# Seven-product attention on one core: the order of maxima, shifts, denominators and the first unit

## The chip, the core and the metric

The kernel runs on one core of a Trainium2 chip. The metric is the device time of one execution in microseconds (us); a comparison takes the median of several executions. Five engines work side by side, each through its own instructions in their written order: TensorE (PE in the profile, with weight loads as PEld), VectorE (DVE), ScalarE (ACT), GpSimd (POOL) and SyncE (SP), which issues most DMAs.

## The reference, cut to what matters

Input x has 4 batches of 256 channels on 64 x 64 points (N = 4096), in float32. A layer of self-attention is followed by a block of clustering, MLP and pointwise convolution:

```python
xf = x.reshape(B, C, N)                              # 4, 256, 4096
q = einsum("oc,bcn->bno", wq, xf) + bq               # 32 wide
k = einsum("oc,bcn->bon", wk, xf) + bk[None, :, None]
attn = softmax(einsum("bnd,bdm->bnm", q, k), axis=-1)
v = einsum("oc,bcn->bon", wv, xf) + bv[None, :, None]
x = gamma[0] * einsum("bcn,bmn->bcm", v, attn).reshape(B, C, H, W) + x
...
y = x + ls1 * cluster(group_norm(x))                 # 4 heads, 2 x 2 folds, 4 centres
y = y + ls2 * conv1x1(gelu(conv1x1(group_norm(y), w1, b1)), w2, b2)   # 256 -> 1024 -> 256
z = relu(batch_norm(y * dw_w))
out = relu(batch_norm(conv1x1(z, pw_w)))
```

The change touches the attention and the seam to what follows it.

## The kernel before

For each batch the 4096 queries are cut into 8 blocks `nb` of 512, and for each block the 4096 keys into 8 groups `g` of 512. A pair is a *unit* `u = 8 * nb + g`, so a batch has 64 units. A unit's scores, exponentials and products are kept in a tile `s` of four quarters (`B21, B11, B12, B22`). The product of exponentials and values is made by a scheme of Strassen's kind: seven products of quarter matrices instead of eight. `factors(u)` forms the sums of quarters that it needs (`t31` on VectorE, `s[:, B12]` and `t4s` on GpSimd), and with them the sums of the softmax's denominators (`acc`: `one` and `both`). `weigh(u, av, part)` (lines 646 to 670) issues the seven products in four parts, in the order that the tables `ORDER` and `LAST` (lines 44 and 45) give; `LAST` holds for a batch's last unit. Product 1 needs `s[:, B11]`, 2 and 3 `s[:, B21]` and `s[:, B22]`, 5 and 7 need `t31`, 6 `s[:, B12]`, and 4 `t4s`. Banks `av` 0 and 1 lie in `ps_a`, 2 and 3 in `ps_m`.

Everything is written by hand in one order per engine (`manual_schedule`); no scheduler moves anything. While unit `u` is weighed, `exps(u + 1)` subtracts the block's maximum (line 589, VectorE) and takes exponentials (lines 593 to 595, ScalarE), `factors(u + 1)` follows, and up to three half units of *scores* of about eleven units ahead are made (`half`, lines 458 to 475): two matmuls into a PSUM tile `sc`, a copy of it into `s` by ScalarE (`kept`, line 439), and a running maximum over keys by VectorE (`highest_of`, line 450). The scores' pool `ps_s` has two buffers, and one of them is `hold`, which keeps the maximum row and the exponentials of B12.

A block's maximum is finished in steps. `fold` (line 507) takes the maximum of the two halves of `top`; it was called by `due` (line 868), right after the last half unit of a block. `highest` (line 557, called at `g == 5`) transposes and reduces on VectorE, copies four small pieces on ScalarE (line 544), reduces and transposes once more, and sends the row through DRAM by two DMAs on SP's queue (`everywhere`); `known` (line 572) copies it into `hold` at `g == 6`. In `weighting` (line 878) the second and third steps of `highest` stood ahead of the maximum of the half unit that was made in the same part:

```python
if ripe:
    next(peak)
    mb = next(peak)
for f in maxima:
    f()
```

At the end of a block `evict` copies the four banks out on ScalarE and scales them with gamma; `combined` adds the quarters on GpSimd during the next block. The first product of the next block writes bank 0, which `evict` must have read. `total` and `leave` divide by the denominators. For the last block of a batch (`more` is false) this was different: `gather` (line 672) ran on GpSimd after three additions of `factors`, VectorE combined the evicted banks 0 and 1 and took banks 2 and 3 straight from PSUM (`complete`), and the denominators were summed over the partitions by four matmuls `den` (line 1005). Then follow a reciprocal, `seen` and `pooled` (statistics and cell sums of x), the division, `add_one`, and a group norm.

In the last ten units of a batch x is loaded again (`load`), v's bias is added on ScalarE (`shift`, line 760, two operations of 128 x 1024 each), and the attention's output is added to it by accumulating DMAs on GpSimd's queue (`back`, `back_one`), from `tail`. `shift` stood ahead of the first products of its unit.

Batch 0 has no predecessor to hide its start in: `alone` (line 803) makes projections and the first block's scores; `derived` makes twelve tiny VectorE operations for later stages, all in unit 0; `wf` turns a small weight.

Of the kernel before, what the change touches and what calls it, by code (L numbers as in the profile page):

```python
# [11 lines left out]
ALU = mybir.AluOpType  # L12
# [7 lines left out]
NBLK = N // NB  # L20
# [22 lines left out]

ORDER = (1, 5), (2, 3), (7, 6), (4,)
# [15 lines left out]
def attention_then_cluster_block(  # L60
# [179 lines left out]
    def derived():  # L240

        for s, e, g, m, b_ in (
            (dw_d, dw_e, "dw_g", "dw_m", "dw_b"),
            (pw_s, pw_e, "pw_g", "pw_m", "pw_b"),
        ):
            nc.vector.tensor_tensor(s, s, par(g), ALU.mult)
            nc.vector.tensor_tensor(e, s, par(m), ALU.mult)
            nc.vector.tensor_tensor(e, par(b_), e, ALU.subtract)
        nc.vector.tensor_tensor(dw_d, dw_d, par("dw_w"), ALU.mult)
        nc.vector.tensor_tensor(lsb1, par("ls2"), par("mlp_b2"), ALU.mult)  # L250
        nc.vector.tensor_tensor(lsb1, lsb1, dw_d, ALU.mult)
        nc.vector.tensor_tensor(dw_e, dw_e, lsb1, ALU.add)

        nc.vector.tensor_scalar(gbv, gbv, pvc("gamma"), None, ALU.mult)
        nc.vector.tensor_scalar(ab, pv_s[:, PV["alpha"] : PV["alpha"] + 2], 0.5, None, ALU.mult)

# [54 lines left out]
    def attention(b, xs, ys):  # L311
# [245 lines left out]
        def highest(nb):  # L557

            top = tops.pop(nb)
# [40 lines left out]
        def factors(u):  # L600
# [15 lines left out]
            plus(t4s[u], s[:, B12], s[:, B21])  # L616
            if g == 0:
# [28 lines left out]
        def weigh(u, av, part):  # L646
# [14 lines left out]
            for i in (ORDER if u < units - 1 else LAST)[part]:  # L661
# [10 lines left out]
        def gather(nb):  # L672

            acc = accs.pop(nb)
            rdens[nb] = work.tile([P, NB], F32, tag="rden", bufs=1, name=f"rden_{b}_{nb}")
            for h in range(2):
                plus(rdens[nb][:, h * QW : (h + 1) * QW], acc[:, 1 - h, 0], acc[:, 1 - h, 1])
# [18 lines left out]
        def combine(nb, eng):  # L696

            t = ts[nb]
            yield eng.tensor_tensor(t[:, 1], t[:, 1], t[:, 0], ALU.subtract)
# [3 lines left out]

        def combined(nb):

            t = ts[nb]
            yield from combine(nb, nc.gpsimd)
            yield nc.gpsimd.tensor_tensor(t[:, ::3], t[:, ::3], ts.pop((nb, 2)), ALU.add)
            yield nc.gpsimd.tensor_tensor(t[:, 1], ts.pop((nb, 3))[:, 0], t[:, 1], ALU.subtract)

        def complete(nb, av, c):

            t = ts[nb]
            dst, src, op = (
# [1328 lines left out]
```

## Time and profile before

| | us |
|---|---|
| median of 3 runs | 3188.45 (3188.23 to 3193.07) |
| time of the profiled execution | 3184.64 |
| its span, first to last instruction | 3182.5 |
| mean granted TensorE clock | 0.992 |
| span of one block of 8 units (187.58 to 245.02) | 57.44 |

| engine, line | what | count | mean ns |
|---|---|---|---|
| PE L664 | products of the weighing, 128x256 | 7168 | 380 |
| PE L426 | scores, 128x512 | 1024 | 467 |
| DVE L589 | subtraction of the maximum, 128x1024 | 512 | 1209 |
| DVE L450 | running maximum, 128x1024 from PSUM | 350 | 1219 |
| DVE L612 | t31, 128x1024 | 256 | 1218 |
| ACT L439 | copy of scores, 128x1024 | 512 | 1010 |
| ACT L760 | shift of x, 128x1024 | 32 | 1137 |
| POOL L598 | additions of 128x512 | 960 (the three largest groups and acc<-t,t) | 1296 to 1402 |

Busy times overlap, since the engines run side by side, and matmuls overlap each other (a mean of 380 ns stands for a new one each 216 ns). What counts is where the engine that is never done waits, and for whom; the views below show that.

### The profile page before, as it was taken

To read this page: it belongs to the slowest core of one execution; us is meant where nothing else is said; L and a number is where in the kernel's file an instruction comes from. 1 tells how busy PE (TensorE), PEld (TensorE's weight loads), DVE (VectorE), ACT (ScalarE), POOL (GpSimd) and SP (SyncE) were. 2 spreads that over 40 slices of the span, in tenths; PEclk is the share of its full clock that TensorE was granted. 3 is DMA by queue.
4 is the path that set the end of the run, shared out by engine and by line. 5 is a ranking of instruction groups with operands and counts; after the bars stand their busy time and mean duration, and the time that the engine had idled before them with its cause. 6 is when DMAs were issued, how large, how long until landed. Compare 5 with 4: busy or idle time off the path is not lost.

```text
span 3182.5 us, 41287 instructions
## 1 busy us (share of the span) xinstructions
PE 3049.3 (96%) x14210; PEld 2501.5 (79%) x14210; DVE 2489.0 (78%) x3569; ACT 1770.9 (56%) x2807; POOL 2315.4 (73%) x2223
## 2 busy tenths in 40 slices
PE   7999999999999999999999999999999999999999
PEld 5788887788678888878867888886877788875786
DVE  4888887777788887777778888777768888877675
ACT  4566664545556666354455666635555666644444
POOL 3888887377578888647758888855866888894663
PEclk9999999999999999999999999999999999999999
DMA  5122226200112113510011212441011112150000
GB/s 165 40 63 64 60 59 185 70 17 27 47 48 66 54 60 98 152 57 17 27 57 44 64 60 59 114 128 57 27 40 44 54 60 63 57 145 6 14 21 27
DMA packets 105873, 200.39 MB, mean 63 GB/s; under 512 B 14416, under 2 KB 30400, under 8 KB 104128
## 3 DMA queue, kind: packets, MB, share of 16 engines
q1 hardware_dynamic: 101856, 181.94, 18.1%
q0 software_dynamic: 2976, 14.70, 2.5%
q8 instruction: 113, 1.85, 0.3%
q10 hardware_dynamic: 832, 1.11, 0.1%
q14 instruction: 96, 0.79, 0.1%
HBM read 149.37 MB, written 48.34 MB: 62 GB/s over the span
## 4 chain that ended last, share of the span: by engine, by line
PE 63%; DVE 14%; POOL 12%; ACT 6%; issue 4%; DMA 1%; SPq 0%; ACTq 0%; POOLq 0%; DVEq 0%
PE av L664 25%; PE mo L1655 9%; PE sc L426 5%; POOL acc L598 5%; PE hq L1738 5%; DVE top L450 3%; DVE s L589 3%; PE hp L1738 3%; PE hr L1738 3%; PE fv L1227 3%; POOL t L598 3%; PE vp L381 2%; ACT s L439 2%; DVE t L612 2%; POOL s L598 1%
## 5 line engine op out<-in xcount | busy, mean ns | idle before, releaser
L439 ACT COPY s<-sc 128x1024 f32<-128x1024 f32 x512 | 514.3, 1010 | 458.1 <-PE sc L426 406.7
L589 DVE TENSOR_TENSOR s<-s,hold 128x1024 f32<-128x1024 f32 x512 | 598.9, 1209 | 8.4 <-ACT hold L572 5.1
L598 POOL TENSOR_TENSOR acc<-acc,t 128x512 f32<-128x512 f32 x416 | 543.7, 1328 | 0.0
L598 POOL TENSOR_TENSOR s<-t,s 128x512 f32<-128x512 f32 x256 | 344.7, 1347 | 268.2 <-DVE t L612 201.1
L664 PE MATMUL av<-s,v 128*128 128x256 f32 x2048 | 529.0, 381 | 10.9 <-ACT t L689 10.9
L664 PE MATMUL av<-t,v 128*128 128x256 f32 x2048 | 529.5, 381 | 4.7 <-DVE t L612 3.8
L664 PE MATMUL av<-s,sum 128*128 128x256 f32 x2048 | 527.3, 380 | 2.6 <-POOL s L598 2.4
L612 DVE TENSOR_TENSOR t<-s,hold 128x1024 f32<-128x1024 f32 x256 | 311.7, 1218 | 217.9 <-POOL acc L598 83.2
L426 PE MATMUL sc<-q,k 128*128 128x512 f32 x1024 | 392.3, 467 | 59.7 <-DVE top L450 38.8
L450 DVE TENSOR_TENSOR top<-sc,top 128x1024 f32<-128x1024 f32 x350 | 426.6, 1219 | 27.0 <-ACT s L439 22.5
L664 PEld LDWEIGHTS av<-s,v 128*128 128x128 f32 x2048 | 389.2, 190 | 73.6 <-ACT t L689 12.5
L664 PEld LDWEIGHTS av<-t,v 128*128 128x128 f32 x2048 | 390.4, 191 | 63.8 <-DVE t L612 5.4
L664 PEld LDWEIGHTS av<-s,sum 128*128 128x128 f32 x2048 | 389.2, 190 | 58.6 <-POOL s L598 5.8
L1693 ACT ACTIVATE hs<-hs,pv_s 128x256 f32<-128x256 f32 x496 | 232.6, 503 | 352.4 <-DVE hs L1729 352.4
L1655 PE MATMUL mo<-hs,w 128*128 128x256 f32 x1512 | 384.8, 381 | 0.0
L598 POOL TENSOR_TENSOR t<-s 128x512 f32<-128x512 f32 x256 | 331.8, 1296 | 58.2 <-PE av L664 46.6
L1655 PEld LDWEIGHTS mo<-hs,w 128*128 128x128 f32 x1512 | 283.8, 190 | 46.8 <-ACT hs L1693 6.1
L593 ACT ACTIVATE hold<-s 128x512 f32<-128x512 f32 x256 | 154.2, 602 | 255.8 <-DVE s L589 255.3
L426 PEld LDWEIGHTS sc<-q,k 128*128 128x128 f32 x1024 | 173.8, 189 | 144.2 <-DVE top L450 84.0
L595 ACT ACTIVATE s<-s 128x1024 f32<-128x1024 f32 x256 | 266.8, 1042 | 0.0
L1729 DVE TENSOR_TENSOR hs<-hq,hs 128x256 f32<-128x256 f32 x496 | 198.2, 420 | 86.3 <-PE hq L1738 76.3
L664 PE MATMUL av<-t,sum 128*128 128x256 f32 x1024 | 262.4, 378 | 0.0
(292 smaller groups left out, 4813.1 us busy)
## 6 DMA issues: line engine op xcount, KB each, us to landing
k<-k SPq DMA_DIRECT2D x256, 256.0 KB, 2.7
x<-in_x SPq DMA_DIRECT2D x62, 512.0 KB, 6.8
out<-xn SPq DMA_DIRECT2D x62, 256.0 KB, 2.1
att<-t SPq DMA_DIRECT2D x56, 256.0 KB, 3.8
x<-att POOLq DMA_DIRECT2D x12, 1024.0 KB, 9.7
q<-q SPq DMA_DIRECT2D x32, 256.0 KB, 4.0
w<-in_w SPq DMA_DIRECT2D x8, 1024.0 KB, 11.1
k<-hl_k SPq DMA_DIRECT2D x28, 256.0 KB, 2.6
```

Source lines behind the costliest of these rows:

```text
L426: nc.tensor.matmul(sc[:, r, :], k_s[:, (2 * h + r) * P : (2 * h + r + 1) * P], qs[u // GRP], start=True, stop=True,)
L439: nc.scalar.copy(slots[u][:, PAIR[h]].rearrange("p h r n -> p r h n"), tiles(sc))
L450: nc.vector.tensor_tensor(top, src, top if saved[nb] is None else saved[nb], ALU.max)
L589: nc.vector.tensor_tensor(sh, sh, mb.to_broadcast([P, 2, 2, QW]), ALU.subtract)
L595: nc.scalar.activation(s[:, PAIR[1]], s[:, PAIR[1]], AF.Exp)
L598: nc.gpsimd.tensor_tensor(out, x, y, op)
L612: nc.vector.tensor_tensor(t31[u], s[:, B11 : B22 + 1 : 2], b12.to_broadcast([P, 2, 2, QW]), ALU.add)
L664: nc.tensor.matmul(av[bank][:, half_ * QW : (half_ + 1) * QW], a[:, r], t[:, r], start=(g == 0 and r == 0 and i in (1, 7, 2, 4)), stop=(g ...
L1655: return nc.tensor.matmul(bank[:, half * HB : (half + 1) * HB], a[:, j], t, start=start, stop=stop)
L1693: nc.scalar.activation(src, src, AF.Gelu_apprx_tanh, bias=pvc("b1", P, j + 4 * (i > 1)))
L1729: nc.vector.tensor_tensor(dst, ps, term, ALU.add)
L1738: nc.tensor.matmul(out, w, x, start=True, stop=True)
```

## The change

Seven edits, all of order or of the engine that does a thing:

- The maximum of the half unit stands ahead of the second and third steps of `highest`.
- From block 2 on, `fold` is called by `highest`, so that it follows the next unit's subtractions.
- `shift` moves to the end of its unit, ahead of `tail`.
- In the last block of a batch VectorE sums the denominators: `factors` of the last unit adds `t31` and takes the difference on VectorE, `gather` adds `t4s` and the halves there too. Banks 2 and 3 are evicted by ScalarE; GpSimd makes the four combining additions and VectorE the last two.
- A table `FIRST` orders unit 0 of each batch: products 1 and 2, then 3 and 5.
- The twelve operations of `derived` are done one a unit from unit 16 on.
- In `alone`, `wf` and two pairs of v stand earlier, and the last maximum precedes its copy.

```diff
--- before.py
+++ after.py
@@ -41,6 +41,7 @@
 
 
 
+FIRST = (1, 2), (3, 5), (7, 6), (4,)
 ORDER = (1, 5), (2, 3), (7, 6), (4,)
 LAST = (1, 5), (7, 6), (2, 3), (4,)
 
@@ -239,21 +240,27 @@
 
     def derived():
 
+        def op(*a):
+            return lambda: nc.vector.tensor_tensor(*a)
+
+        def scale(*a):
+            return lambda: nc.vector.tensor_scalar(*a)
+
+        todo = []
         for s, e, g, m, b_ in (
             (dw_d, dw_e, "dw_g", "dw_m", "dw_b"),
             (pw_s, pw_e, "pw_g", "pw_m", "pw_b"),
         ):
-            nc.vector.tensor_tensor(s, s, par(g), ALU.mult)
-            nc.vector.tensor_tensor(e, s, par(m), ALU.mult)
-            nc.vector.tensor_tensor(e, par(b_), e, ALU.subtract)
-        nc.vector.tensor_tensor(dw_d, dw_d, par("dw_w"), ALU.mult)
-        nc.vector.tensor_tensor(lsb1, par("ls2"), par("mlp_b2"), ALU.mult)
-        nc.vector.tensor_tensor(lsb1, lsb1, dw_d, ALU.mult)
-        nc.vector.tensor_tensor(dw_e, dw_e, lsb1, ALU.add)
-
-        nc.vector.tensor_scalar(gbv, gbv, pvc("gamma"), None, ALU.mult)
-        nc.vector.tensor_scalar(ab, pv_s[:, PV["alpha"] : PV["alpha"] + 2], 0.5, None, ALU.mult)
-
+            todo.append(op(s, s, par(g), ALU.mult))
+            todo.append(op(e, s, par(m), ALU.mult))
+            todo.append(op(e, par(b_), e, ALU.subtract))
+        todo.append(op(dw_d, dw_d, par("dw_w"), ALU.mult))
+        todo.append(op(lsb1, par("ls2"), par("mlp_b2"), ALU.mult))
+        todo.append(op(lsb1, lsb1, dw_d, ALU.mult))
+        todo.append(op(dw_e, dw_e, lsb1, ALU.add))
+        todo.append(scale(gbv, gbv, pvc("gamma"), None, ALU.mult))
+        todo.append(scale(ab, pv_s[:, PV["alpha"] : PV["alpha"] + 2], 0.5, None, ALU.mult))
+        return todo
 
     def wf():
 
@@ -556,6 +563,7 @@
 
         def highest(nb):
 
+            fold(nb)
             top = tops.pop(nb)
             low = spare()[:, nb % 2]
             steps = reduced(top[:, 0], top[:, 1], low, ALU.max, nc.scalar.copy)
@@ -614,6 +622,10 @@
             )
             plus(s[:, B12], t31[u][:, 1], s[:, B11])
             plus(t4s[u], s[:, B12], s[:, B21])
+            if u == units - 1:
+                nc.vector.tensor_tensor(one, one, t31[u][:, 1], ALU.add)
+                nc.vector.tensor_tensor(both, both, one, ALU.subtract)
+                return
             if g == 0:
                 plus(both, s[:, B12], s[:, B21])
             else:
@@ -658,7 +670,7 @@
                 3: (2, 1, s4, s[:, B22]),
             }
 
-            for i in (ORDER if u < units - 1 else LAST)[part]:
+            for i in {0: FIRST, units - 1: LAST}.get(u, ORDER)[part]:
                 bank, half_, a, t = terms[i]
                 for r in range(2):
                     nc.tensor.matmul(
@@ -673,8 +685,13 @@
 
             acc = accs.pop(nb)
             rdens[nb] = work.tile([P, NB], F32, tag="rden", bufs=1, name=f"rden_{b}_{nb}")
+            eng = nc.vector if nb == NBLK - 1 else nc.gpsimd
+            if nb == NBLK - 1:
+                eng.tensor_tensor(acc[:, 1], acc[:, 1], t4s[units - 1], ALU.add)
             for h in range(2):
-                plus(rdens[nb][:, h * QW : (h + 1) * QW], acc[:, 1 - h, 0], acc[:, 1 - h, 1])
+                eng.tensor_tensor(
+                    rdens[nb][:, h * QW : (h + 1) * QW], acc[:, 1 - h, 0], acc[:, 1 - h, 1], ALU.add
+                )
 
         def evict(nb, av, i):
 
@@ -693,29 +710,16 @@
                 scale=pvc("gamma"),
             )
 
-        def combine(nb, eng):
+        def combined(nb, last=nc.gpsimd):
 
             t = ts[nb]
+            eng = nc.gpsimd
             yield eng.tensor_tensor(t[:, 1], t[:, 1], t[:, 0], ALU.subtract)
             yield eng.tensor_tensor(t[:, 3], t[:, 1], t[:, 3], ALU.subtract)
             yield eng.tensor_tensor(t[:, 1], t[:, 1], t[:, 2], ALU.add)
             yield eng.tensor_tensor(t[:, 2], t[:, 2], t[:, 3], ALU.add)
-
-        def combined(nb):
-
-            t = ts[nb]
-            yield from combine(nb, nc.gpsimd)
-            yield nc.gpsimd.tensor_tensor(t[:, ::3], t[:, ::3], ts.pop((nb, 2)), ALU.add)
-            yield nc.gpsimd.tensor_tensor(t[:, 1], ts.pop((nb, 3))[:, 0], t[:, 1], ALU.subtract)
-
-        def complete(nb, av, c):
-
-            t = ts[nb]
-            dst, src, op = (
-                (t[:, ::3], av[2].rearrange("p (h n) -> p h n", h=2), ALU.add),
-                (t[:, 1], av[3][:, :QW], ALU.subtract),
-            )[c]
-            nc.vector.scalar_tensor_tensor(dst, src, pvc("gamma"), dst, ALU.mult, op)
+            yield last.tensor_tensor(t[:, ::3], t[:, ::3], ts.pop((nb, 2)), ALU.add)
+            yield last.tensor_tensor(t[:, 1], ts.pop((nb, 3))[:, 0], t[:, 1], ALU.subtract)
 
         def total(nb):
 
@@ -820,10 +824,19 @@
                     halved("k", 1)
                     halved("q", 1)
                     rest = load_rest()
-                for h in range(2):
-                    half(u, h)()
+                half(u, 0)()
+                if u < GRP - 1:
+                    half(u, 1)()
+                else:
+
+                    sc = products(u, 1)
+                    highest_of(0, tiles(sc))
+                    kept(u, 1, sc)
+                    v_pair(14)
                 if u < 6:
                     v_pair(u + GRP)
+                elif u == 6:
+                    wf()
                 if u > 1:
                     next(rest, None)
             fold(0)
@@ -832,15 +845,12 @@
                     f()
             tp = turned_over(0, ps_m.tile([P, 4, P], F32, tag="m", name=f"tt_{b}_0"))
             half(GRP, 0)
-            v_half(28)
             dgs["dg"] = across(0, "w2", tp)
             spread(0, dgs["dg"])
+            v_pair(15)
             exps(0)
             factors(0)
-            v_half(29)
-            v_pair(15)
             half(GRP, 1, True)
-            wf()
             for f in sums(GRP - 1):
                 f()
 
@@ -871,8 +881,8 @@
                 return []
             p, h, kept_only = at[u, part]
             fs = [half(p, h, kept_only)]
-            if h and p % GRP == GRP - 1:
-                fs.append(lambda: fold(p // GRP))
+            if p == 2 * GRP - 1 and h:
+                fs.append(lambda: fold(1))
             return fs
 
         def weighting(next_x, fill, early, begin):
@@ -932,13 +942,11 @@
                 elif ripe:
                     peak = highest(nb + 1)
                     next(peak)
-                if u == 0:
-                    early()
+                if early and nb > 1:
+                    early.pop(0)()
                 if u in views:
                     pooled(views[u])
                     seen(views[u], (0,))
-                if u in shifts:
-                    shift(shifts[u])
                 weigh(u, av, 0)
                 if short:
                     two = ps_s.tile([P, 2, NB], F32, tag="s", name=f"tt_{b}_{nb + 1}")
@@ -954,28 +962,22 @@
                 if g == GRP - 1:
                     evict(nb, av, 0)
                     evict(nb, av, 2 if more else 1)
-                    if not more:
-                        for _ in combine(nb, nc.vector):
-                            pass
                 if g + 1 < GRP or more:
                     factors(u + 1)
                 if more and nb and g == GRP - 2:
                     known(mb)
+                for f in maxima:
+                    f()
                 if ripe:
                     next(peak)
                     mb = next(peak)
-                for f in maxima:
-                    f()
                 if (u, 0) not in at or (u, 1) in at:
                     caught(1)
                 if u in views:
                     seen(views[u], (1,))
                 weigh(u, av, 2)
                 if g == GRP - 1:
-                    if more:
-                        evict(nb, av, 1)
-                    else:
-                        complete(nb, av, 0)
+                    evict(nb, av, 1 if more else 2)
                 if short:
                     spread(nb + 1, dgs["dg"])
                 for f in due(u, 3):
@@ -989,15 +991,19 @@
                 weigh(u, av, 3)
                 if g == 3 and nb + 2 < NBLK:
                     q_block(nb + 2)
-                if g == GRP - 1 and more:
+                if g == GRP - 1:
                     evict(nb, av, 3)
-                    quarters = combined(nb)
+                    quarters = combined(nb, nc.gpsimd if more else nc.vector)
                 elif nb and g < 3:
                     for _ in range(2):
                         next(quarters)
+                if u in shifts:
+                    shift(shifts[u])
                 tail(u)
 
             nb = NBLK - 1
+            for _ in range(4):
+                next(quarters)
             table(AF.Sqrt)
             two = ps_s.tile([P, 2, NB], F32, tag="s", name=f"den_{b}_{nb}")
             den, inv = two[:, 0], two[:, 1]
@@ -1009,10 +1015,11 @@
                     start=True,
                     stop=True,
                 )
-            complete(nb, av, 1)
             fill(2)
             rec = work.tile([P, P], F32, tag="top", bufs=1, name=f"rec_{b}_{nb}")
             nc.vector.reciprocal(rec, den[:, :P])
+            for _ in quarters:
+                pass
             seen(nb - 1)
             pooled(nb - 1)
             for j in range(4):
...
-                next_x, fill, (lambda: None) if b else derived, begin
+                next_x, fill, [] if b else derived(), begin
```

## The prediction

> **What bounds the kernel now.** I read the busy shares, then TensorE's waits in order of time, then at each wait the timelines of all engines. Each timeline line gives start and length in us; in brackets is the idle time before it and what ended it.
>
> ```profile
> PE 3049.3 (96%) x14210; PEld 2501.5 (79%) x14210; DVE 2489.0 (78%) x3569; ACT 1770.9 (56%) x2807; POOL 2315.4 (73%) x2223
> ```
>
> TensorE is the bound. 133 us of the 3182.5 are without a matmul; only those, and stretches at half clock, can be won. Waits recur at the same places of each batch. First kind, units 13 and 14 of batch 0:
>
> ```profile
> 185.36 1.03 PE L664 MATMUL av<-t,v 128*128 128x256 f32 x4
> 187.58 0.73 PE L426 MATMUL sc<-q,k 128*128 128x512 f32 x2 [1.20 <-DVE top L450]
> ...
> 184.36 1.22 DVE L612 TENSOR_TENSOR t<-s,hold 128x1024 f32<-128x1024 f32 x1 [0.94 <-ACT s L595]
> 185.94 0.25 DVE L547 TENSOR_REDUCE few<-few 32x16 f32<-32x64 f32 x1 [0.36 <-ACT few L544]
> 186.22 0.20 DVE L554 STREAM_TRANSPOSE few<-few 32x32 f32<-32x32 f32 x1
> 186.35 1.17 DVE L450 TENSOR_TENSOR top<-sc,s 128x1024 f32<-128x1024 f32 x1
> ```
>
> One score buffer is free beside `hold`, so the scores of unit 25 wait until VectorE has taken the maximum of unit 24, and that stands behind two small steps which wait for ScalarE. The same wait of 1.2 us ends at 245.02, 302.48, 359.93 and 417.39: five a batch.
>
> Second kind, at the head of block 7 (unit 56), in batches 0 and 1:
>
> ```profile
> 487.51 1.13 PE L664 MATMUL av<-s,v 128*128 128x256 f32 x4 [2.72 <-ACT t L689]
> ...
> 1278.31 1.27 POOL L598 TENSOR_TENSOR t<-s 128x512 f32<-128x512 f32 x1 [1.97 <-PE av L664]
> ...
> 1271.03:1274.44 3.41, 3.41 (x10) 2.70 (x9) 0.77 (x1) 3.41 (x6) 3.33 (x4) 0.50 1.01 210
> ```
>
> TensorE waits until ScalarE has copied block 6 out of PSUM, behind a shift of x. In batches 1 to 3 the clock then falls to 0.50 for 3.41 us, and GpSimd in its turn waits 1.97 us for TensorE. Third kind, the end of a batch:
>
> ```profile
> 533.51 1.13 PE L664 MATMUL av<-s,sum 128*128 128x256 f32 x4
> ...
> 536.21 1.03 PE L664 MATMUL av<-t,v 128*128 128x256 f32 x4
> 539.75 0.41 PE L1005 MATMUL den<-rden,ones 128*32 128x128 f32 x4 [2.51 <-POOL rden L598]
> 541.18 3.37 PE L381 MATMUL vp<-wv_s,x 128*128 128x256 f32 x8
> ...
> 531.86 1.59 POOL L598 TENSOR_TENSOR s<-t,s 128x512 f32<-128x512 f32 x1
> 533.54 1.26 POOL L598 TENSOR_TENSOR t<-s 128x512 f32<-128x512 f32 x1
> ...
> 536.34 1.37 DVE L700 TENSOR_TENSOR t<-t 128x256 f32<-128x256 f32 x1
> ```
>
> The denominators wait for GpSimd's five additions after t4. The 533.51 line begins 0.05 after GpSimd's s is done at 533.45: GpSimd, without a pause from 494 on, is level with TensorE here.
>
> **What the Trainium skill says.** "TensorE: Matmul & The Clock Gate", Part 1, says that the array is gated to half clock when it was idle over a window of about 3.4 us. The windows above agree (0.50 for 3.41 us), though a wait of 2.5 to 2.7 us was enough here, and not always (not at 487.51). "SBUF — State Buffer", section "SBUF: two separate sides", says that a VectorE operation with two SBUF inputs and a GpSimd one that reads SBUF lock each other out. The trace agrees: the 1.37 us addition above runs beside GpSimd's, where GpSimd's pace sets it.
>
> **Part by part.** Sums are made on the span of 3182.5; that run took 3184.64, 3.8 under the median of 3188.45, and I take the same difference off the median.
>
> *Maximum ahead, folding behind.* Nothing is added. The fold (0.69) now follows the two subtractions, so they, the exponentials and t of unit 14 come 0.65 earlier: t ends at 184.9 instead of 185.58. ScalarE's copy of the scores, which the maximum waits for, ends near 184.9 too (scores end 183.79, copy 1.0). The maximum runs 184.9 to 186.1; TensorE wants the buffer at 187.58 - 1.20 = 186.38. The wait goes whole: 20 x 1.21 = **24.2**. Late next are the small steps, 186.4 to 186.7 instead of 186.42. The maximum row they send landed 1.3 us (batch 0, block 2) or about 2.1 us (later blocks) before ScalarE read it; TensorE being 1.2 earlier, 0.7 or a little less is left in the later blocks, and at block 2 ScalarE may wait 0.2, with 1.5 us of idle time behind it. GpSimd idles 6 to 7.6 us in such a block, so it follows.
>
> *Shifts of x last.* Four pairs of 1.14 us change place on ScalarE alone. The evictions of block 6 start when the exponentials end; with the hold row ahead of the first shift too (1.28 us earlier for VectorE's subtractions), the first is done near 484.3 and TensorE, free at 484.8, need not wait. But GpSimd must then feed it. Its chain from unit 55 on gains only what t of unit 55 gains: 0.65. So TensorE is held again, in pieces of about 1 us in units 59 to 61, and s of unit 63 comes 0.65 earlier plus 0.2 of a small wait: 0.85 in batch 0. In batches 1 to 3 GpSimd's own wait of 1.97 also goes, as TensorE is no longer late at unit 56: 0.65 + 1.97 = 2.6. Together 0.85 + 3 x 2.6 = **8.7**. The shift of x_1 now delays exponentials of unit 57 by some 0.85; their t ends near 491.4, TensorE wants it at 491.6. GpSimd's accumulating DMAs wait for the shifts: x_1 is done near 488.1, its DMA is reached at 491. SP's queue keeps its order.
>
> *VectorE sums, GpSimd combines.* Five GpSimd additions (534.76 to 540.56) leave the path; VectorE makes the two that need no t4 beforehand, then one of 0.7 and two of 0.42 while TensorE does its last three products. Denominators follow the last product at once. From the end of s (S): products 3.5, den 0.85, reciprocal 0.95, the two late additions that used to lie before it 1.15, statistics and cells 2.5, the multiplication 1.2, two additions 1.35, statistics and their sum 1.9: S + 13.4. Before, S = 533.45 and the group norm's matmul at 550.57: 17.1. TensorE's projections, at full clock if the 2.51 us wait is gone, fit inside. That is 3.7, less the lock: VectorE's adds beside GpSimd's cost 0 (they find pauses) to 1.2 (each waits a GpSimd addition). I take 0.6: 3.1 in batches 0 to 2 = **9.3**. In batch 3 GpSimd turns weights before it combines, and VectorE's 1.15 of late additions eat the 1.28 that the denominators win (waits 0.83 and 0.45 at 2870): **0**.
>
> *Start (batch 0).* The twelve tiny operations stood 4.75 us ahead of t of unit 1 and made waits of 0.91 (84.95) and 1.43 (91.43); one a unit from unit 16 on, they fit in VectorE's pauses of 0.4 to 1.15 before each t. The transposition of `wf` leaves the wait of 1.92 (74.50), the last maximum no longer waits for ScalarE (0.6), and a pair of v fills the wait of 3.42 before the turned maximum. Following the chain, scores of unit 11 come at 87 if the half clock of 59.3 to 69.5 goes, at 88 if not, instead of 91.43: 3.4 to 4.5, I take **3.9**.
>
> *Other first unit.* In batches 1 to 3 t is awaited 0.96 us at 860.50, and the order now puts another product there. But the scores after it wait for the second score copy:
>
> ```profile
> 858.51 1.02 PE L664 MATMUL av<-s,v 128*128 128x256 f32 x4
> 860.50 1.13 PE L664 MATMUL av<-t,v 128*128 128x256 f32 x4 [0.96 <-DVE t L612]
> 861.48 0.73 PE L426 MATMUL sc<-q,k 128*128 128x512 f32 x2
> ...
> 860.42 1.01 ACT L439 COPY s<-sc 128x1024 f32<-128x1024 f32 x1
> ```
>
> The copy ends at 861.43, the scores start at 861.48, with either order. Value **0** (up to 0.1 each).
>
> Sum: 24.2 + 8.7 + 9.3 + 3.9 = 46.1, less about 2 for the two early VectorE adds of each batch, which can hold up s of unit 63 (0 to 0.9 each): **44**. 3188.45 - 44 = **3144**.
>
> **Rivals.**
> 1. *GpSimd does not bind block 7.* Then TensorE gets the whole 2.72 back, and 1.7 more (half of 3.41) in three batches: 2.72 + 3 x 4.4 = 15.9 instead of 8.7: 3137. For: it waits at most 0.23 there now. Against: it has no pause of its own.
> 2. *Half of each 1.2 stays*, because the maximum then waits for ScalarE's copy: 20 x 0.6 = 12 back, and VectorE's sums are paced by GpSimd's lock, 1.2 x 3 more: 3160. For: 0.3 us is all the margin. Against: the copy starts as soon as the scores end.
> 3. *Slower: the maximum row comes late.* Small steps later, TensorE earlier: the subtraction, then the exponentials, then the first product of the next block wait, 24 times. Exponentials are done 3.2 us before their use, so it begins to cost at 0.7 + 3.2 = 3.9 us of lateness and outweighs 44 when it costs 1.85 each, at 5.7. At 6.5 it costs 24 x 2.6 = 62: 3206. The row takes 3.3 to 4.2 us now; nothing new is put ahead of it.
> 4. *The waits only move*, so that the span stays: 3188. Against: TensorE is the bound of blocks 1 to 6, where GpSimd is 85 to 88% and VectorE 81 to 87% busy (stretches of 100 us from 200 to 500).
>
> **How the numbers follow.** The forecast has 0.67, its own range 3136 to 3154; rival 1 0.10, rival 2 0.15, rival 3 0.04, rival 4 0.04. 3133 to 3163 holds the first three cases. 0.2%, or 6 us, is what a measurement can tell from no change: faster 0.92, same 0.04, slower 0.04.
>
> **What would show it.** Scores after the small steps start without a wait of 1.2 (rival 2: 0.5 left). At the head of block 7 no wait for ScalarE's evictions, no 0.50 clock, but waits for GpSimd of about 1 us later in it; without these, rival 1. Denominators without a wait for GpSimd, and VectorE's statistics directly ahead of the group norm's matmul; batch 3 unchanged there. At 861 the scores at the same distance from the first product. A late row would show as ScalarE's hold copy waiting for a DMA. Wrong is the forecast if the tail is longer than S + 15, or if the blocks 1 to 6 last more than 56.5 us instead of 57.46.

## The result, and the profile after

The changed kernel takes 3173.92 us (median of 6 runs, 3166.91 to 3181.04), the kernel before 3190.91 beside it (6 runs). The ratio is 0.9943, with an interval of 0.9925 to 0.9961: about 17 us faster, where 44 were forecast, and outside the range of 3133 to 3163.

The two profiled executions understate this, since that of before took 3184.64, less than any of these six, and that of after is its slowest (3181.04, span 3179.1): their spans differ by 3.4. The spread of the six goes with the granted clock: its mean is 0.995 in the fastest and 0.991 in the slowest, worth some 13 of the 14 us between them (an estimate, from 0.004 of 3174). The profiles are used for places, the medians for sums. Both traces, cut at the same TensorE instructions:

| stretch (us) | forecast | before | after | difference |
|---|---|---|---|---|
| scores of unit 7 (second half) to unit 22, batch 0 | -3.9 | 107.04 | 106.05 | -1.0 |
| unit 22 to unit 63, batch 0 | -6.05 | 293.00 | 299.01 | +6.0 |
| the same, batch 1 | -6.05 | 293.28 | 290.30 | -3.0 |
| the same, batch 2 | -6.05 | 293.94 | 290.27 | -3.7 |
| the same, batch 3 | -6.05 | 293.04 | 299.08 | +6.0 |
| unit 63's scores to the end of its s, batches 0 to 3 | -0.85, 3 x -2.6 | 74.0 to 78.0 | 73.4 to 76.7 | -0.5, -2.2, -2.2, -1.3 |
| from there to the group norm, batches 0 to 3 | 3 x -3.1, 0 | 17.11, 17.18, 17.20, 15.50 | 13.43, 14.16, 13.23, 15.29 | -3.7, -3.0, -4.0, -0.2 |

The last rows came out nearly as forecast. The first part of the change, the largest term of the sum, did not: it gained half of its 6 us in two batches and lost 6 in the other two. TensorE's row of the scores in the page of before, then the busy shares and the same row in the page of after (busy us and mean ns, then the idle time before them and what ended most of it):

```profile
L426 PE MATMUL sc<-q,k 128*128 128x512 f32 x1024 | 392.3, 467 | 59.7 <-DVE top L450 38.8
```

```profile
PE 3063.0 (96%) x14210; PEld 2503.5 (79%) x14210; DVE 2508.3 (79%) x3573; ACT 1778.2 (56%) x2815; POOL 2315.7 (73%) x2219
...
L433 PE MATMUL sc<-q,k 128*128 128x512 f32 x1024 | 395.3, 471 | 58.5 <-DMA k<-k 27.0
```

The scores still stand idle for 58.5 us, but no longer for VectorE's maximum above all: 27.0 of it now ends with the landing of a k tile. TensorE's busy time has grown by 14 us for the same number of instructions, in part from a lower clock. TensorE's timeline in block 1 of batch 0, where the row of block 2 is made (start, length, what, idle time before it):

```profile
186.75 0.73 PE L433 MATMUL sc<-q,k 128*128 128x512 f32 x2
...
192.97 1.03 PE L676 MATMUL av<-t,v 128*128 128x256 f32 x4
195.85 0.47 PE L433 MATMUL sc<-q,k 128*128 128x512 f32 x1 [1.86 <-DMA k<-k]
```

The scores of unit 25 start with no wait, as forecast. The first scores of unit 26 wait 1.86. Their k tile is loaded on SP's queue (SPq). That queue before and after, in the same block:

```profile
186.45 0.32 SPq L98 DMA_DIRECT2D row_mx<-few  x1
187.83 0.32 SPq L99 DMA_DIRECT2D mr<-row_mx  x1
188.25 2.60 SPq L750 DMA_DIRECT2D att<-t  x2
190.94 8.64 SPq L404 DMA_DIRECT2D k<-k  x3
```

```profile
187.11 0.32 SPq L99 DMA_DIRECT2D row_mx<-few  x1
190.17 0.32 SPq L100 DMA_DIRECT2D mr<-row_mx  x1
190.58 0.90 SPq L754 DMA_DIRECT2D att<-t  x2
191.57 1.13 SPq L411 DMA_DIRECT2D k<-k  x2
```

SP works in order. The second DMA of the maximum row reads what the first wrote, so SP stands until the first has landed, and the stores of `att` and the k tile stand behind it. Before, the k tile landed at 194.44, just ahead of its use at 194.60. After, the row leaves 0.66 later, takes 3.0 us to land instead of 1.3, and the tile lands at 195.72; TensorE would have taken it at 194.0. The load itself also took 4.15 us instead of 3.50.

This block is the tightest, but the others show the same. In all 20 blocks with such a wait the scores now start 0.14 us after their k tile has landed. They wait 1.39 to 2.18 us in the seven blocks with a late row (together 13.0) and 0.08 to 0.85 in the 13 others (together 4.2). Before, the tile was there 0.16 to 1.51 us ahead of its use, 1.25 in the median: about the 1.2 us that TensorE was to gain.

Why does the same DMA of 2 KB take 3.0 us? It does so in three blocks of batch 0 and four of batch 3 (2.6 to 3.1), and 1.3 in the other 17. The DMA queues in the 3.2 us from the row's start (packets, MB, share of the engines; then the issues with us to landing):

```profile
q8 instruction: 1, 0.02, 2.5%
q1 hardware_dynamic: 32, 0.00, 0.7%
...
row_mx<-few SPq DMA_DIRECT2D x1, 2.0 KB, 3.0
```

Beside the row's 32 small packets there is one of 16 KB, an instruction fetch, which starts at 187.79 and takes 1.26. In the trace's packets 15 of the 16 pieces of the row have started by 188.06, and the last starts at 189.03, when the fetch ends. In all seven late rows such a packet starts 0.5 to 0.8 us after the row, in none of the others. In the trace of before it came 2.2 to 2.3 us after the row in the same blocks. The twelve traces of this case hold 288 rows, 38 of them late. In each of the 38 a fetch begins 0.5 to 1.2 us after the row, and the last piece starts within 0.02 us of that fetch's end; no row on time has a fetch there. The wait of that piece is not the whole delay: the landing follows 1.0 to 1.2 us after the last piece, where it is 0.3 to 0.4 in the rows on time. Where these 0.7 us go is not shown. The page counts 113 of these packets; 28,420 matmuls and weight loads make 251 to each.

The Trainium skill bears this out: "Runtime: NRT & Kernel Launch", section "Instruction fetch mechanics", says that an engine's instructions are refilled in blocks of 16 KiB, 256 instructions, over a DMA queue of its own, and calls the cost mostly hidden. "DMA: Bandwidth & Descriptors", section "Queues, rings and completion order", says that a DMA engine changes between queues only at packet boundaries. The trace agrees, except that the cost is not hidden here.

After such a wait the array may drop to half clock. From 312 us (length, PE busy with instructions, PEld, DVE, ACT, POOL, granted clock, DMA share, GB/s):

```profile
312.00:315.46 3.46, 1.28 (x6) 0.82 (x5) 2.86 (x3) 0.59 (x1) 3.38 (x4) 1.00 0.69 236
315.46:318.87 3.41, 3.41 (x10) 2.73 (x9) 1.50 (x3) 3.00 (x4) 3.25 (x4) 0.50 0.00 0
```

A wait of 2.18 ending at 314.77 brought 3.41 us at 0.50, 1.7 us of work lost on top of the wait. "TensorE: Matmul & The Clock Gate", Part 1, names a window of about 3.4 us for this; its length agrees, but 2.2 us of waiting sufficed.

A second loss is in batch 0 alone. VectorE, GpSimd and TensorE at 242 us:

```profile
242.86 2.10 DVE L244 TENSOR_TENSOR pw_e<-pc_s,pw_e 128x2 f32<-128x2 f32 x1
244.88 1.21 DVE L620 TENSOR_TENSOR t<-s,hold 128x1024 f32<-128x1024 f32 x1
246.01 1.21 DVE L457 TENSOR_TENSOR top<-sc,s 128x1024 f32<-128x1024 f32 x1
```

```profile
242.59 2.35 POOL L746 TENSOR_TENSOR t<-t,rden 128x1024 f32<-128x1024 f32 x1
```

```profile
247.27 0.74 PE L433 MATMUL sc<-q,k 128*128 128x512 f32 x2 [2.03 <-DVE top L457]
```

One of the twelve tiny operations, 128x2, lasts 2.10 us: it ends together with GpSimd's division of 2.35 us (line 746), which it runs beside. The maximum behind it is late, and TensorE waits 2.03 us. At the head of block 7 the wait of 2.72 is gone, and short waits for GpSimd stand further on in the block. They are far smaller than the pieces of about 1 us that the prediction had; that GpSimd sets the pace is read from its own row, which has no pause above 0.3 us from 484 to the end of s at 539.03. TensorE's timeline of batch 0 there, and then at the batch's end:

```profile
527.88 1.13 PE L676 MATMUL av<-s,sum 128*128 128x256 f32 x4 [0.38 <-POOL s L606]
529.24 1.13 PE L676 MATMUL av<-t,v 128*128 128x256 f32 x4 [0.23 <-POOL t L606]
```

```profile
541.78 1.03 PE L676 MATMUL av<-t,v 128*128 128x256 f32 x4
542.74 0.91 PE L1011 MATMUL den<-rden,ones 128*32 128x128 f32 x8
...
552.46 0.38 PE L289 MATMUL gnm_gn<-mv_gn,left 128*128 128x1 f32 x2 [0.81 <-DVE mv_gn L287]
```

The denominators follow the last product without a wait for GpSimd, and the group norm waits for VectorE's statistics: S is 539.03, so this is S + 13.43, forecast S + 13.4.

### The profile page after: what moved, and what is told of

Same layout as the page of the kernel before. It is cut to its first block, busy times and chain, and to the rows that moved or that the text cites. A ratio compares the mean times of both kernels' runs of the same rounds, so it can differ in the third digit from the quotient of the medians.

```text
span 3179.1 us, 41316 instructions
## 1 busy us (share of the span) xinstructions
PE 3063.0 (96%) x14210; PEld 2503.5 (79%) x14210; DVE 2508.3 (79%) x3573; ACT 1778.2 (56%) x2815; POOL 2315.7 (73%) x2219
## 4 chain that ended last, share of the span: by engine, by line
PE 65%; POOL 13%; DVE 10%; DMA 5%; issue 3%; ACT 3%; SPq 0%; POOLq 0%; ACTq 0%; DVEq 0%
PE av L676 27%; PE mo L1662 9%; PE sc L433 6%; PE hq L1745 5%; POOL acc L606 4%; DMA k<-k 3%; PE hp L1745 3%; PE hr L1745 3%; PE fv L1234 3%; POOL t L606 3%; DVE top L457 2%; POOL s L606 2%; PE vp L388 2%; DVE s L597 2%; PE mo L1646 1%
## 5 line engine op out<-in xcount | busy, mean ns | idle before, releaser
L433 PE MATMUL sc<-q,k 128*128 128x512 f32 x1024 | 395.3, 471 | 58.5 <-DMA k<-k 27.0
```

The source lines that it names most:

```text
L433: nc.tensor.matmul(sc[:, r, :], k_s[:, (2 * h + r) * P : (2 * h + r + 1) * P], qs[u // GRP], start=True, stop=True,)
```

## The experiments

Ten kernels, each with a few lines changed against one of the two. Ratios are to the kernel before, run beside them on the same chip. "The stretch of unit 22 to 63" is that of the table above, from the first scores of the one unit to those of the other.

**k_first**: the changed kernel, k tile ahead of the row on SP's queue.

```diff
-            if u + 1 < units:
+            if u + 1 < units and u + 1 not in ks:
                 k_unit(u + 1)
...
                 if ripe:
+                    if u + 13 < units:
+                        k_unit(u + 13)
                     next(peak)
                     mb = next(peak)
```

> The changed kernel with one edit: in the six blocks that send a maximum row, the load of the k tile that is needed next stands ahead of the row on SP's queue instead of behind the row and the two stores of att. Theory A (the new wait is the k load, stuck behind the row on SP): the 27.0 us of waits for k go, the stretch from the scores of unit 22 to those of unit 63 falls from 299.0 to about 288 in batches 0 and 3 and from 290.3 to about 288 in batches 1 and 2, together some 26 us: span about 3153, median about 3148 to 3155. The row may still take 3 us to land. Theory B (the wait for k only stands where another would be, GpSimd's or the maximum row's own): the waits for k go but others of the same size take their place, span 3170 or more.

Measured: 3154.99 (3152.88 to 3162.81), ratio 0.9894 (0.9881 to 0.9908), 34 us below before. SP's queue, the same block:

```profile
176.07 7.63 SPq L411 DMA_DIRECT2D k<-k  x2
186.13 0.32 SPq L99 DMA_DIRECT2D row_mx<-few  x1
189.45 0.32 SPq L100 DMA_DIRECT2D mr<-row_mx  x1
```

The k tile of unit 26 is now the second of the two loads in the first line. The row still lands late as in the changed kernel (3.2 us here, seven late ones in all), but it costs little: the stretch of unit 22 to 63 takes 290.3 in batch 3 with four late rows, and 288.9 in batches 1 and 2 with none. Batch 0, at 293.4, keeps the wait of 2.03 at unit 33, and half clock follows it at 245.8. This is theory A, with the median at the upper end of what it stated.

**phase**: the changed kernel, eleven tiny matmuls more at its start.

```diff
+            tick = ps_m.tile([P, NB], F32, tag="m", name="tick")
+            for _ in range(11):
+                nc.tensor.matmul(tick[:, :D], ones, ident[:, :D], start=True, stop=True)
             roots()
```

> The changed kernel with eleven tiny matmuls (128x32, result unused) in front of TensorE's first work, while it waits for x. They do nothing but put 44 more instructions into TensorE's stream, so that its 16 KB instruction fetches, one about every 29 us, come some 5 us earlier against all other work. Theory A (the row lands late in batches 0 and 3 because TensorE's instruction fetch sits on one of the row's DMA engines): the fetch nearest to the row moves from 0.5 to 0.8 us after the row's start to about 4 us before it, all 24 rows land in 1.3 us, and batches 0 and 3 take about 290.3 like batches 1 and 2 from unit 22 to unit 63: span about 3162. Theory B (the row is late for another reason, such as the stores of att or GpSimd): rows of batches 0 and 3 still take 2.6 to 3.1 us, that stretch 299, span 3175 to 3181.

Measured: 3160.89 (3154.66 to 3167.99), ratio 0.991 (0.9895 to 0.9925). All rows of batches 0 and 3 land in 1.3 us. The DMA queues in two windows of 3.2 and 2.9 us from a row's start, the first of batch 0 and the fifth of batch 2:

```profile
q1 hardware_dynamic: 101, 0.14, 15.8%
...
row_mx<-few SPq DMA_DIRECT2D x1, 2.0 KB, 1.3
```

```profile
q8 instruction: 1, 0.02, 2.0%
q1 hardware_dynamic: 32, 0.00, 0.8%
...
row_mx<-few SPq DMA_DIRECT2D x1, 2.0 KB, 2.7
```

In the first no fetch is left, and batch 3 falls from 299.1 to 289.6, batch 0 to 293.3 (with its 2.03 wait). The second was not expected, and settles it: not all 24 rows were on time, the last two of batch 2 were now late (2.7 and 2.8), and just there the fetch had moved to 0.71 and 0.78 us behind the row. 44 unused instructions of TensorE decide which rows are late, so the fetch is TensorE's and it is the cause of the late landing.

**max_only**: the kernel before with the first part alone.

```diff
+            fold(nb)
             top = tops.pop(nb)
...
+                for f in maxima:
+                    f()
                 if ripe:
                     next(peak)
                     mb = next(peak)
-                for f in maxima:
-                    f()
```

(and `due` calls `fold` for block 1 only)

> The kernel before with nothing but the first part of the change: maximum ahead of the small steps, fold behind the subtractions. The prediction on record would have 24.2 us less, about 3166. Theory A (the wait goes over to the k load behind the row): the stretch from unit 22 to unit 63 is as in the changed kernel, 299 in batches 0 and 3 (6 more), 290.3 in batches 1 and 2 (3 less), so that the sum is about +5: 3185 to 3197.

Measured: 3185.03, ratio 0.9988 (0.9982 to 0.9995): 4 us, not 24. This is the lower end of what theory A stated. The same seven rows are late as in the changed kernel, so the first part by itself brings the row and the fetch together. The stretch of unit 22 to 63 takes 294.4, 289.9, 289.9 and 300.0; batch 0 was expected at 299, but has neither the wait at unit 33 nor half clock. TensorE's row of the scores:

```profile
L426 PE MATMUL sc<-q,k 128*128 128x512 f32 x1024 | 393.1, 468 | 53.2 <-DMA k<-k 23.9 <-DVE top L450 14.1 <-ACT s L439 7.7
```

**no_max**: the changed kernel with that edit undone.

> The changed kernel with that first part undone, all others kept. Theory A: the stretch from unit 22 to unit 63 is 293 in all batches as before and no wait for k is left; what remains is the gain of the other parts, about 9 us in the profiled spans: median 3178 to 3183. The prediction on record would have it 24 above the changed kernel: 3198.

Measured: 3172.86, ratio 0.9947 (0.9935 to 0.996), the same as the changed kernel: as made, the first part is worth nothing within the intervals. The stretch takes 293.0 to 293.8 in all batches, all rows land in 1.3 us, and the old wait is back:

```profile
L433 PE MATMUL sc<-q,k 128*128 128x512 f32 x1024 | 392.3, 467 | 63.8 <-DVE top L457 38.2 <-DMA k<-k 11.0 <-ACT s L446 9.5
```

The time is 5 us below what was expected, since the profiled spans had understated the other parts.

**k_before**: the edit of k_first in the kernel before.

> The kernel before, with nothing but the k load put ahead of the maximum row, as in k_first. Theory A (in the kernel before the k load came 0.2 to 0.7 us ahead of its use, so nobody waited for it; it binds only once the 1.2 us wait is gone): unit 22 to unit 63 takes 293 in all four batches as before, the five waits of 1.2 us stay, and the median is within 3 us of before. Theory B (the order on SP's queue is worth time by itself, and k_first owes its gain to that): 8 us or more below before, 3182 or less.

Measured: 3188.82, ratio 0.9998 (0.999 to 1.0006). This is theory A: alone the order on SP's queue is worth nothing. With the first part it is worth 16 us by the ratios (0.9943 to 0.9894) and 19 by the medians, which were not taken side by side.

**k_early**: k_first, with the tiny operations kept out of units with `g == 5`.

```diff
-                if early and nb > 1:
+                if early and nb > 1 and g != 5:
```

> The kernel of k_first, in which the twelve tiny operations of derived skip the units with g == 5. Theory A (the wait of 2.03 us of the scores of unit 33, in batch 0 alone, comes from the tiny operation of unit 21: it shares SBUF with GpSimd's long multiplication of leave and lasts 2.1 us instead of 0.2, ahead of t and the maximum): that wait goes, batch 0 from unit 22 to unit 63 falls from 293.4 to about 290, and the median by 3 to 4 us against k_first, to about 3151. Theory B (VectorE is late in that block for another reason): the wait of 2 us stays and so does the time, 3155.

Measured: 3156.62, ratio 0.9894 (0.988 to 0.9909). VectorE around the row of the same block:

```profile
240.00 0.69 DVE L545 TENSOR_REDUCE few<-top 128x16 f32<-128x512 f32 x1
240.60 1.21 DVE L620 TENSOR_TENSOR t<-s,hold 128x1024 f32<-128x1024 f32 x1
```

The wait of 2.03 is gone and batch 0 falls from 293.4 to 290.3, half of it the half clock that followed the wait, as theory A has it; in the median (3154.99 with, 3156.62 without) these 3 us do not show. The place is settled, its worth in the whole is not.

**k_start**: k_early, and in the start of batch 0 the old order of unit 0 and a later pair of v.

```diff
-            for i in {0: FIRST, units - 1: LAST}.get(u, ORDER)[part]:
+            for i in {0: FIRST if b else ORDER, units - 1: LAST}.get(u, ORDER)[part]:
...
-            v_pair(15)
             exps(0)
+            v_pair(15)
```

> The kernel of k_early with two more edits in the start of batch 0: unit 0 of batch 0 uses the old table ORDER, and the last pair of v is issued behind the first exponentials instead of ahead of them. The stretch from the scores of unit 7 (second half) to unit 22 took 107.0 in both profiles with the old start, and 106.1, 106.1, 103.3 and 103.3 in those with the new one. Theory A (FIRST puts the scores of unit 9 behind two products, and ScalarE's copy of them then stands behind the exponentials of unit 1, the wait of 1.51 at 81.93; the copy of v holds the exponentials of unit 0 back where the array is at half clock): the stretch takes 102 to 104.5, and the median is 1 to 2 below k_early, about 3149. Theory B (the start is bound by VectorE's and GpSimd's work anyway): 103.3 or 106.1 as before, no difference.

Measured: 3154.76 (3152.6 to 3159.13), ratio 0.9889 (0.9873 to 0.9905). The stretch of the start, from unit 7 to unit 22, takes 104.6 with half clock from 64.8 to 71.6, where k_first and k_early, also with half clock there, took 106.1 and 105.8: 1.1 to 1.5 better, just outside the 104.5 stated. In the median it can't be told apart, and the 3149 expected was missed by 6.

**k_start_tick**: k_start with six tiny matmuls at the start.

> The kernel of k_start with six tiny matmuls (result unused) ahead of TensorE's first work, 24 instructions, which move its instruction fetches about 2.7 us ahead of the rest. Theory A (with the k load ahead of it, a late row still costs about 0.3 each, through later exponentials): all 24 rows land in 1.3 us, batches 0 and 3 take 288.5 to 289.5 from unit 22 to unit 63 like batches 1 and 2, and the median is 1 to 3 below k_start: about 3152. Theory B (once the k load is ahead of it the row's landing costs nothing): the rows land in 1.3 us, but the stretch stays at 289 to 290.4 and the median at 3154 to 3155.

Measured: 3154.25 (3151.84 to 3155.76), ratio 0.989 (0.9875 to 0.9905). 23 of 24 rows land in 1.3 us; the first of batch 3 takes 3.05, and the fetch stands 0.71 behind it. The stretch of unit 22 to 63 takes 289.1 to 289.3 in all batches, against 288.9 to 290.4 in k_start. The median does not move, as theory B has it. With the k tile ahead, a late row costs little: in k_start 0.2 to 0.6 us in each of the three late blocks of batch 0, up to 0.3 in those of batch 3.

**tail_only**: the kernel before with the edit of the last block alone.

```diff
+            if u == units - 1:
+                nc.vector.tensor_tensor(one, one, t31[u][:, 1], ALU.add)
+                nc.vector.tensor_tensor(both, both, one, ALU.subtract)
+                return
...
-                    if more:
-                        evict(nb, av, 1)
-                    else:
-                        complete(nb, av, 0)
+                    evict(nb, av, 1 if more else 2)
...
-                    quarters = combined(nb)
+                    quarters = combined(nb, nc.gpsimd if more else nc.vector)
```

(with `gather` on VectorE too, as in the change)

> The kernel before with nothing but the edit of a batch's last block: VectorE sums the denominators, ScalarE evicts all four banks, GpSimd combines. The prediction on record has 3.1 each in batches 0 to 2 and nothing in batch 3, together 9.3: median about 3179 to 3180. Theory A (the term is right; the profiles show 3.0 to 4.0 from the end of GpSimd's s of unit 63 to the group norm in batches 0 to 2, 0.2 in batch 3): 3178 to 3180. Theory B (the gain is given back in the pointwise stage behind it): no more than 3 us, 3186 to 3189.

Measured: 3179.80, ratio 0.9964 (0.9946 to 0.9981), 10.7 us. From the end of s to the group norm 3.3, 3.9, 3.8 and 0.2 less. This is theory A.

**shift_only**: the kernel before with the shifts of x alone at the end of their units.

```diff
-                if u in shifts:
-                    shift(shifts[u])
                 weigh(u, av, 0)
...
+                if u in shifts:
+                    shift(shifts[u])
                 tail(u)
```

> The kernel before with nothing but the shifts of x moved to the end of their units. The prediction on record has 8.7. Theory A (what TensorE gains at the head of block 7, 2.7 to 2.9 a batch, it loses again to GpSimd later in that block, wholly in batch 0 and by 0.6 to 1.8 in the others): from the scores of unit 63 to the end of s of unit 63 the four batches take about 0.2, 1.9, 1.9 and 0.9 less, together 5: median about 3184. Prediction's own number: 3180. Theory B (GpSimd gives nothing back): 11 to 12 less, 3177.

Measured: 3182.05, ratio 0.9971 (0.9961 to 0.9982), 8.5 us, between theory A's 3184 and the prediction's 3180. In the profile (3177.65, the second fastest of the eight executions) the batches take 0.1, 1.9, 1.8 and 1.8 less from unit 63's scores to the end of its s, together 5.7. The rest lies where nothing was changed: from there to the group norm 1.6 to 1.7 less in batches 0 to 2. The denominators still wait 2.5 us for GpSimd there, but the half clock that followed in before (at 540.6, 1325.6 and 2110.7) did not come. The last section suggests that this depends on where the wait falls, and not on the shifts; then other executions of the same kernel can have it.

## Why the prediction was wrong, point by point

*Maximum ahead, folding behind* (forecast 24.2). This is the step that failed: "The wait goes whole: 20 x 1.21 = 24.2 ... Late next are the small steps". The wait did go, but late next was the k tile of the following unit. The prediction followed the maximum row forward, to ScalarE's copy and the exponentials, and asked what stands ahead of the row on SP's queue ("nothing new is put ahead of it"). It did not ask what stands behind it. The profile of before had the answer: the k tile landed 0.16 to 1.51 us ahead of its use, and TensorE was to become 1.2 us faster. The prediction also took the row's own time as fixed ("The row takes 3.3 to 4.2 us now", which is its second DMA, 3.2 to 4.7 in the trace). The first, 1.3 us in all 24 rows before, took 2.6 to 3.1 in the seven that now met TensorE's instruction fetch. max_only and no_max show the part worth 4 us and nothing; phase shows the fetch; k_first shows that the queue order is what makes TensorE pay. The prediction's own sign of being wrong came too: from the scores of unit 25 to those of unit 33 it is 60.5 us in batch 0, where 56.5 was its limit.

The 24.2 can be followed, as an estimate. Of it 17.2 come back as waits for k, some 5 as later scores that no view lists (next paragraph), 5.1 as half clock after three of the waits (at 315.5, 2510.3 and 2687.7), and 2.0 as the wait at unit 33: together 29, so that the four stretches should be 5 longer. They are 5.4 longer (1178.7 against 1173.3).

Even with the queue mended the term is too large: k_early has 15.1 less than before in the four stretches, not 24.2. In batch 1 of k_start 5.6 us of visible waits are gone, but each of the five scores behind the mended ones (units 26, 34, 42, 50, 58) comes 0.25 later against its neighbours: unit 26 starts at 968.40, when VectorE ends the maximum of unit 25 at 968.35. Such a wait is not listed as idle, since the matmuls' modelled ends overlap it. Twenty of these make 5 us.

*Shifts of x last* (forecast 8.7): 6.2 in the changed kernel's profile, 8.5 in the median of shift_only. The reason was right (GpSimd, without a pause, sets the end of the block), and the half clock at 1271, 2056 and 2814 is gone. The term was 0.4 too large in batches 0 to 2 and 1.3 in batch 3, where two GpSimd steps just ahead of unit 63's s took 1.63 and 1.70 us instead of 1.16 and 1.27. The 2 us that the prediction took off its sum, for VectorE's early additions, cover most of that.

*VectorE sums, GpSimd combines* (forecast 9.3): 10.9 in the profile, 10.7 alone. Right, batch 3's zero too. But it can't simply be added to the last part: the half clock at 540.6, 1325.6 and 2110.7 is missing in the profile of either alone, worth 1.6 us each time. Here the wait ahead of it is gone; in shift_only the wait is still there.

*Start* (forecast 3.9, half clock left open as 3.4 to 4.5). The stretch was 1.0 shorter in the changed kernel and 0.9 in k_first, and 3.8 and 3.7 in no_max and phase, where the order of this stretch is the same: in the changed kernel half clock lies at 66 to 73 us, while no_max has none in the start and phase 3.41 us of it, over at 63.5 (from the matmuls that fill `hold` to the next scores it is 2.47 and 2.48 us there instead of 4.90). With little or no half clock the gain is 3.7 to 3.8 where up to 4.5 was stated; with 6.8 us of it, 1.0 where 3.4 was. The order of the start was read rightly, the price of the clock was not. The step "they fit in VectorE's pauses of 0.4 to 1.15" failed: they are tiny, but one of them met GpSimd's division and took 2.10, and cost batch 0 of k_first some 3 us (k_early).

*Other first unit* (forecast 0): from the first product of a batch to the scores of its unit 13 it is 26.36 before and 26.37 after in batch 1, alike in 2 and 3. Right.

*Rivals.* Rival 3 had the row come late, and it does: ScalarE's copy waits 7.9 us for it in seven blocks. But its price was put on the exponentials, which stay covered (within 0.6 us in k_start, where nothing else hides it); the price was paid through the k tile, which no rival named. Rival 4, waits that only move, is what the first part did by itself.

Open: the other parts add up to about 16 us (no_max) of the 20 forecast, and k_first makes 34 of the 44, so that the first part with the queue mended is worth about 18 of 24. Which parts lack the last few us is not settled. A stretch that no edit touches differs between profiles as well: from the group norm behind batch 3's attention to the end it is 302.9 to 307.1 us in the twelve. The changed kernel has the 307.1, with 6.8 us of half clock at its head (2872). Why one execution meets it and another does not was not followed.

## What to carry to other kernels

When a wait on the bounding engine is taken away, everything that used to be just in time becomes late by as much: list each transfer with less slack than the gain, and look on every in-order queue behind an instruction that waits, not only ahead of it. A DMA that needs another's landing belongs behind the loads that do not, where it holds nobody up. And a small DMA has two durations, one of them set by when an instruction fetch of the busiest engine passes: give it slack, or expect the time to change with edits that have nothing to do with it.

## What had not been expected of the hardware

- A fetch of 16 KB of TensorE's instructions, one for about 250 instructions, took 0.9 to 1.4 us in the changed kernel. A 2 KB DMA that starts 0.5 to 1.2 us ahead of it lands after 2.6 to 3.2 us instead of 1.3 (all twelve traces); one of its 16 pieces starts only when the fetch ends.
- With eleven unused matmuls at the start the changed kernel takes 3160.89 instead of 3173.92 (ratios 0.991 and 0.9943). In the profiles 15 us of it lie in batches 0 and 3, where the rows are now on time, and 3 in the start, where the clock is higher.
- A VectorE operation on 128x2 took 2.10 us beside a GpSimd operation of 2.35.
- Waits of 2.0 to 2.2 us were enough for 3.41 us of half clock at some places (those that end at 314.77, 2510.28 and 2686.69), while 2.5 us were not at another (541.36 in shift_only), nor 3.33 us at 2856.78 in the changed kernel. The traces' clock records suggest why. All half clock starts on a grid of 3.413 us: in the changed kernel at 66.31, 315.49 (73 steps on) and 615.86 (88 more). The three short waits lie in one step of the grid, with 2.18, 2.11 and 2.03 us; the others are cut by it, into 1.84 and 0.68, and 1.55 and 1.78. Of all 61 waits above 1.7 us of products, scores and denominators from 100 us on, in the twelve traces, each of the 34 with 2.0 us or more in one step is followed by half clock, and six of the other 27. No experiment moved a wait across the grid by design.
